# Rotary attention and routed feed-forward on one core: the row sums, their inverses and the division move by one step, and the kept copies of the feed-forward get fixed places

## The chip, the core and the metric

The kernel runs on one core of one Trainium2 chip. The metric is the device time of one execution in microseconds, and the figure given for a kernel is the median of its runs. Five engines work side by side, each with its own instruction stream in order: TensorE (PE, with its weight loads shown as PEld), VectorE (DVE), ScalarE (ACT), GpSimd (POOL) and SyncE (SP), which here only issues DMAs. They wait for each other through semaphores.

## The reference

The input is x, four sequences of 512 tokens with 512 features, all in fp32. It is normalised (layer norm), and two branches are added to x:

```python
def _L0_attn_ref(x, W_DQ, W_UQ, W_QR, W_DKV, W_UK, W_UV, W_KR, W_O):   # H=16, D_H=128, D_HR=64
    c_Q = x @ W_DQ.T                       # latent of 128
    q_C, q_R = heads(c_Q @ W_UQ.T), rope(heads(c_Q @ W_QR.T))
    c_KV = x @ W_DKV.T                     # latent of 128
    k_C, v = heads(c_KV @ W_UK.T), heads(c_KV @ W_UV.T)
    k_R = rope(x @ W_KR.T)                 # one for all heads
    scores = clip([q_C, q_R] . [k_C, k_R], -80, 80)
    weights = softmax(causal(scores) / sqrt(192))
    return (weights @ v) @ W_O.T

def _L0_ffn_ref(x, ...):                   # 7 experts of 512, top 3, and one shared
    output = (silu(x @ Ws1) * (x @ Wsg)) @ Ws2
    for e in range(7):
        output += ((silu(x @ W1[e]) * (x @ Wg[e])) @ W2[e]) * w_e[..., None]

x = x + attn(xn) + ffn(xn)
```

## The kernel before

The kernel has two large stages. First comes the feed-forward: norm, gate and shared expert, then the routed tokens, sorted by expert and cut into units of 512 rows. After it comes the attention, 16 heads of 4 sequences.

**Feed-forward.** A unit is three 512x512x512 products, called h, g and y. `product` does each with seven block products (a Strassen scheme) instead of eight, in the order `ORDER = (0, 1, 5, 4, 6, 2, 3)`; each is four matmuls. They go to three PSUM banks, `BANK = (0, 1, 2, 0, 2, 0, 0)`. A block product that another needs later is copied by ACT from its bank to SBUF (`kept`): product 0 gives v1, product 5 gives v2, product 4 gives v5 and product 6 gives v3. The bank is free for the next block product only after that copy. The copies live in one pool tag `v` with five buffers. In h, DVE adds v1, v2, v3 and v5 to other banks and ACT applies silu. In y, v1, v3 (with v5 added), v2 and a fourth tile v4 are stored by SP to DRAM (`y_d`), in the order v1, v3, v2, v4. A buffer that y stored is free again when that store has landed. The pool hands buffers out in the order in which they become free in the program. By the addresses of the built program, the h of the next unit gets these: v1 the buffer of y's v1, v2 that of y's v5 (which isn't stored), v5 that of y's v3, v3 that of y's v2. ACT runs in order, so a copy that waits for a buffer holds up those behind it.

**Attention.** The loop runs over 32 steps i; a step is one pair of heads of one sequence. The kernel works in latent space. Step i does:

- `scores(i)` on PE: score blocks without rotation (line 1432), then the rotary part onto them (line 1443). Banks: `a0`, `a1` for the first key block, `c` and one of the `pj` pool for the third, `b0` and `b1` for the second and fourth.
- `rotary_query(i+1)` (pqr, line 1282) and `query(i+1, 0)` (pq, line 1297) on PE for the next step.
- `weights(i)`: DVE clips the banks to SBUF (line 1461, six instructions), ACT takes exp (line 1465), POOL multiplies by the triangular mask (line 1469) and adds up key blocks into the tiles su (lines 1493 and 1497).
- `rope` on DVE for the next query: one product with cos and four with sin (lines 1268 and 1271), and a subtraction on POOL (line 1272).
- `values(i-1, j)` on PE (av, line 1513), copied by ACT into og.

A group q is four heads, those of steps 2q and 2q+1. For a group:

- `sums(q)`: four matmuls with ones (line 1532) into bank `a0` give the row sums, and DVE inverts them (line 1534, rc).
- `spread_by_dma(q)`: SP issues 16 DMAs of 64 KB that copy rc to four tiles rb of 128 partitions (line 1544).
- `divide(q)`: DVE multiplies og by the four rb (line 1566) and forms the block sums for the seven-product scheme (lines 1572 and 1575).
- `project_out(q)`: the product with the folded output weights m (op, line 230), 28 matmuls in seven block products into banks `b1`, `c` and `b0`. ACT copies some banks (line 1605), POOL adds the copies to acc (line 1612), and DVE adds three banks to acc (line 1615): bank `c` after the second block product, banks `b0` and `b1` at the end. `combine(g)` (line 1677, three DVE instructions) adds the routed rows of one token tile to acc; it stands right behind the first bank sum. `fetch` gathers the rows for a later combine with indirect DMAs from POOL (line 1664).

`keep` fixes the program's order on each engine for most instructions. So the order on DVE within two steps is what the source says. In the kernel before, with i even: clips, inverse of group i/2-1, rope, first bank sum, combine, two bank sums. With i odd: clips, rope, divide. `sums` stands behind pq of even steps, `project_out(q)` at the end of even step 2q+4.

Of the kernel before, what the change touches and what calls it, by code (L numbers as in the profile page):

```python
# [18 lines left out]
P = 128  # L19
# [23 lines left out]
def kernel(  # L43
# [87 lines left out]
    def rows(src):  # L131
        return src.rearrange("(c p) f -> p c f", p=P)

    def ffn_in(at, name, w, x_of, between, step=FC):

        hp = fps.tile([P, S], F32, tag="h", name=f"h_{name}")
        gp = fps.tile([P, S], F32, tag="g", name=f"g_{name}")
        for ps, wt in ((hp, w[0]), (gp, w[1])):
            for f in range(FC):
                for c in range(DC):  # L140
                    keep(
                        nc.tensor.matmul(
                            ps[:, ts(f, P)],
                            wt[:, c, ts(f, P)],
                            x_of(c),
                            start=(c == 0),
                            stop=(c == DC - 1),
                        )
                    )
            if ps is hp:  # L150
                between()
        sl = sw.tile([P, S], F32, tag="v", name=f"sl_{name}", bufs=5)
        keep(nc.scalar.activation(sl, hp, AF.Silu))
        cols = [t.rearrange("p (c n) -> p c n", c=FC) for t in (gp, sl)]

        for f in range(0, FC, step):
            keep(nc.vector.tensor_mul(*(t[:, f : f + step] for t in (at, *cols))))
        return at
# [113 lines left out]
    def block(t):  # L272
        if len(t.shape) > 2:
            axes = " ".join("abc"[: len(t.shape) - 1])
            t = t.rearrange(f"p {axes} -> p ({axes})")
        return t.rearrange("p (j f) -> p j f", j=2)
# [11 lines left out]
    def product(name, tag, a, w, done, hooks):  # L288

        banks = banks_of(tag, name)

        def kept(i, k):
            t = sw.tile([P, D], F32, tag="v", name=f"v{i}_{name}", bufs=5)
            keep(nc.scalar.copy(block(t), banks[k]))  # L297
            return block(t)

        copies = {0: (1, 0), 5: (2, 0), 4: (5, 2), 6: (3, 0)}  # L300
        sums = {1: 1, 2: 2, 3: 0}

        def then(p):
            if p in copies:
                done(copies[p][0], kept(*copies[p]))
            else:
                done(-p, banks[sums[p]])
            if p in hooks:
                hooks[p]()

        seven(a, w, banks, then, keep)
# [720 lines left out]
    def unit_out(s, a, w, hooks):  # L1032
        def to(t, n):
            at = (s * TPB + 2 * t) * P
            return y_d[at : at + 2 * P, half[n]].rearrange("(j p) f -> p j f", p=P)

        v = {}

        def done(i, src):
            v[i] = src  # L1040
            if i == -1:
                keep(V.tensor_add(v[1], src, v[1]))
                load_in(to(0, 0), v[1])
            elif i == 3:
                keep(V.tensor_add(v[3], v[3], v[5]))
                load_in(to(1, 1), v[3])
            elif i == -2:
                keep(V.tensor_add(v[2], src, v[2]))
                load_in(to(0, 1), v[2])
            elif i == -3:  # L1050
                t = block(sw.tile([P, D], F32, tag="v", name=f"v4_r{s}", bufs=5))
                keep(nc.scalar.copy(t, src))
                load_in(to(1, 0), t)

        product(f"yr{s}", "y", a, w, done, hooks)
# [324 lines left out]
    with tc.If(used < SURE + 1) as few:  # L1380
        at = act_tile("few").rearrange("p c (t f) -> p t c f", t=TPB)[:, 0]
        at = ffn_in(at, "few", wbuf, lambda c: xT[SURE][:, c, :P], nothing, 1)
        y = sw.tile([P, D], F32, tag="v", name="y_few", bufs=5)
        yp = ffn_out("few", at, wbuf, keep)
        keep(nc.scalar.copy(y[:, half[0]], yp[:, half[0]]))
        keep(nc.vector.tensor_copy(y[:, half[1]], yp[:, half[1]]))
        nc.sync.dma_start(y_d[ts(SURE * TPB, P), :], y)
    with few.Else():
        last[0] = None
# [63 lines left out]
    def weights(i, bank, then, behind):  # L1453

        pt = ap.tile([P, 5 * S], F32, tag="pt", name=f"pt_{i}")

        def clip(to, src):  # L1460
            keep(nc.vector.tensor_scalar(to, src, CLIP, -CLIP, ALU.min, ALU.max))  # L1461

        def exp(t):

            keep(nc.scalar.activation(t, t, AF.Exp, scale=QK_SCALE))  # L1465

        def mask(t, at, k=1, step=P):
            m = t[:, at : at + P]
            keep(nc.gpsimd.tensor_mul(m, m, tri))  # L1469

        for j in range(2):
            a = pt[:, ts(j, S)]
            clip(a, bank[j, 0])
            exp(a)
            mask(pt, PT[j, 0])
        half = 2 * P
        for j in (1, 0):
            clip(pt[:, PT[j, 2] : PT[j, 2] + half], bank[j, 2][:, :half])
        exp(pt[:, ts(2, S)])
        for j in range(2):  # L1480
            mask(pt, PT[j, 2])
        then()
        for j in range(2):
            t = pt[:, ts(3 + j, S)]
            clip(t, bank[j, 1])
            exp(t)
            mask(pt, PT[j, 1])
            mask(pt, PT[j, 3])
        behind()
        su = []  # L1490
        for j in range(2):
            t = ap.tile([P, S], F32, tag="su", name=f"su_{i}_{j}", bufs=4)
            keep(nc.gpsimd.tensor_copy(t[:, :P], pt[:, PT[j, 0] : PT[j, 0] + P]))
            for kc in range(1, TPB):
                prev = pt[:, PT[j, 0] + P : PT[j, 0] + S] if kc == 1 else t[:, kc * P :]
                keep(
                    nc.gpsimd.tensor_add(  # L1497
                        t[:, kc * P :], prev, pt[:, PT[j, kc] : PT[j, kc] + PT_W[kc]]
                    )
                )  # L1500
            su.append(t)
        pts[i], sus[i] = pt, su
# [25 lines left out]
    def sums(q):  # L1528

        sb = bank("a0")(f"sb_{q}")  # L1530
        for j, su in enumerate(sus.pop(2 * q) + sus.pop(2 * q + 1)):
            keep(nc.tensor.matmul(sb[ts(j, 32), :], ones[:, :32], su, start=True, stop=True))  # L1532
        rc = ap.tile([P, S], F32, tag="rc", name=f"rc_{q}", bufs=1)
        keep(nc.vector.reciprocal(rc, sb))
        return rc
# [21 lines left out]
    def divide(q):  # L1557

        o = og.pop(q)

        for cols in half if q == n // 2 - 1 else [slice(0, S)]:
            for j, rb in enumerate(spread[q]):
                keep(nc.vector.tensor_mul(o[:, j, cols], o[:, j, cols], rb[:, cols]))  # L1566
        a11, a21 = (o[:, 0:2, half[t]] for t in range(2))
        a12, a22 = (o[:, 2:4, half[t]] for t in range(2))
        x = [ap.tile([P, 2, S // 2], F32, tag=f"s{k}", name=f"s{k}_{q}") for k in (1, 2, 4)]

        def add(*t):
            keep(nc.vector.tensor_add(*t))

        def sub(*t):
            keep(nc.vector.tensor_sub(*t))

        firsts_of[q] = first_factors(add, sub, a11, a12, a21, a22, *x, a21)
# [104 lines left out]

    factors_of = {0: load_factors(0)}

    for i in range(n):
        more = i + 1 < n
        even = i % 2 == 0
        q = i // 2 - 1  # L1690
        held = scores(i)
        raw_copy, turn_q = rotary_query(i + 1, psum(f"pqr_{i + 1}")) if more else (nothing, nothing)
        qc_copy = query(i + 1, 0, psum(f"pq_{i + 1}_0")) if more else nothing
        weights(i, held, raw_copy, nothing if even else turn_q)
        qc_copy()
        if even and i > 0:
            spread_by_dma(q, sums(q))
        if even:
            turn_q()
        if i > 0:  # L1700
            values(i - 1, 0)
        if more:
            query(i + 1, 1, psum(f"pq_{i + 1}_1"))()
        if i < 2:
            project(2 + i, psum)
        if 1 < i < 5:
            turn_keys((2, 3, 1)[i - 2], psum)
        if i > 0:
            values(i - 1, 1)
        if even and i > 2:  # L1710
            project_out(q - 1, first_added=lambda: combine(q))
        if i == 1:
            combine(0)
        if even and i != 2 or i == 1:
            fetch((i + 1) // 2)
        if not even and i > 1:
            divide(q)

    q = n // 2 - 1

    def last_heads():
        combine(NTT - 1)
        values(n - 1, 0)
        values(n - 1, 1)
        last_rc.append(sums(q))

    last_rc = []
    project_out(q - 1, last_heads)
# [51 lines left out]
```

## Time and profile before

| | |
|---|---|
| Median of 10 runs | 1398.75 us (1387.89 to 1402.6) |
| The profiled execution: its own time / its span | 1386.11 us / 1384.3 us |
| Granted TensorE clock, mean of the span | 0.993 |
| Feed-forward units, 178.98 to 690.43 us: PE busy | 483.23 of 511.45 us |
| Attention loop, 842.09 to 1337.34 us: PE busy | 495.24 of 495.25 us |
| End, 1337.34 to 1384.3 us: PE busy | 42.44 of 46.96 us |

The share of busy time alone says little: matmuls are pipelined and their ends are modelled, so a PE that is shown busy throughout can still take longer than it must for a group of matmuls that waits inside. The median of the runs lies 12.6 us above the profiled execution's own time.

### The profile page before, as it was taken

To read this page: it belongs to the slowest core of one execution; us is meant where nothing else is said; L and a number is where in the kernel's file an instruction comes from. 1 tells how busy PE (TensorE), PEld (TensorE's weight loads), DVE (VectorE), ACT (ScalarE), POOL (GpSimd) and SP (SyncE) were. 2 spreads that over 40 slices of the span, in tenths; PEclk is the share of its full clock that TensorE was granted. 3 is DMA by queue.
4 is the path that set the end of the run, shared out by engine and by line. 5 is a ranking of instruction groups with operands and counts; after the bars stand their busy time and mean duration, and the time that the engine had idled before them with its cause. 6 is when DMAs were issued, how large, how long until landed. Compare 5 with 4: busy or idle time off the path is not lost.

```text
span 1384.3 us, 17913 instructions
## 1 busy us (share of the span) xinstructions
PE 1341.7 (97%) x5949; PEld 995.9 (72%) x5949; DVE 970.8 (70%) x1426; ACT 405.1 (29%) x714; POOL 844.5 (61%) x952
## 2 busy tenths in 40 slices
PE   9999899999999998999999999999999999999998
PEld 8778787788777786768755666666666666666666
DVE  7679455676656576648546877777977777987775
ACT  3234122222223221222223332332332332333231
POOL 5122654554436443343157888888888889888883
PEclk9999999999999999999999999999999999999999
DMA  7841245675557563443331123333123432124332
GB/s 274 207 128 31 78 127 152 166 207 171 172 152 213 160 187 111 126 141 111 99 108 31 46 86 105 107 100 116 54 87 101 137 107 90 48 87 128 107 107 84
DMA packets 174100, 167.90 MB, mean 121 GB/s; under 512 B 57904, under 2 KB 136752, under 8 KB 174000
## 3 DMA queue, kind: packets, MB, share of 16 engines
q1 hardware_dynamic: 161264, 133.10, 32.6%
q0 software_dynamic: 12736, 33.57, 8.1%
q8 instruction: 49, 0.80, 0.2%
q14 instruction: 51, 0.42, 0.1%
HBM read 116.02 MB, written 34.87 MB: 109 GB/s over the span
## 4 chain that ended last, share of the span: by engine, by line
PE 95%; issue 2%; DVE 1%; another core or an unknown queue 1%; ACT 1%; POOL 0%; DVEq 0%; ACTq 0%; POOLq 0%
PE op L230 14%; PE hr L230 11%; PE gr L230 10%; PE yr L230 10%; PE av L1513 10%; PE sb L1432 4%; PE sa L1432 4%; PE pq L1297 4%; PE sa L1443 2%; PE pqr L1282 2%; PE ys L230 2%; PE hs L230 2%; PE gs L230 2%; PE sb L1443 2%; PE sb L1532 2%
## 5 line engine op out<-in xcount | busy, mean ns | idle before, releaser
L182 POOL DMA_INDIRECT xs<-xn_d,idx_i x208 | 226.9, 1091 | 223.3 <-DVE xT L199 164.3
L1469 POOL TENSOR_TENSOR pt<-pt,tri 128x128 f32<-128x128 f32 x256 | 139.7, 566 | 68.7 <-ACT pt L1465 62.0
L1465 ACT ACTIVATE pt<-pt 128x512 f32<-128x512 f32 x160 | 94.4, 628 | 257.8 <-DVE pt L1461 255.2
L1513 PEld LDWEIGHTS av<-pt,xnT 128*128 128x128 f32 x512 | 95.4, 190 | 83.7 <-issue 47.7
L1513 PE MATMUL av<-pt,xnT 128*128 128x512 f32 (+3 forms) x512 | 149.8, 436 | 0.0
L230 PE MATMUL op<-m,og 128*128 128x256 f32 x512 | 118.6, 379 | 0.5 <-DVE og L1566 0.5
L1271 DVE TENSOR_TENSOR swap_q<-qraw,sinT 32x512 f32<-32x512 f32 x128 | 117.7, 920 | 1.7
L1497 POOL TENSOR_TENSOR su<-su,pt 128x256 f32<-128x256 f32 (+1 forms) x128 | 105.2, 822 | 10.0
L230 PEld LDWEIGHTS op<-m,og 128*128 128x128 f32 x512 | 96.0, 190 | 14.5 <-DVE og L1566 1.3
L1461 DVE TENSOR_SCALAR pt<-sa 128x512 f32<-128x512 f32 x64 | 41.0, 681 | 70.6 <-PE sa L1443 70.6
L1664 POOL DMA_INDIRECT yg<-y_d,pos_i x48 | 54.5, 1134 | 56.7 <-issue 50.3
L230 PE MATMUL op<-m,s 128*128 128x256 f32 x384 | 88.2, 379 | 0.1
L1497 POOL TENSOR_TENSOR su<-pt 128x384 f32<-128x384 f32 x64 | 83.8, 1310 | 0.0
L1612 POOL TENSOR_TENSOR acc<-acc,v 128x512 f32<-128x512 f32 x60 | 80.6, 1344 | 5.1 <-ACT v L1605 3.2
L230 PEld LDWEIGHTS op<-m,s 128*128 128x128 f32 x384 | 72.9, 190 | 10.3 <-issue 0.5
L230 PE MATMUL hr<-xT,w 128*128 128x256 f32 x288 | 68.1, 387 | 6.3 <-issue 6.3
L1677 DVE SCALAR_TENSOR_TENSOR acc<-yg,wk,acc 128x512 f32<-128x512 f32 x48 | 56.7, 1181 | 19.1 <-POOL acc L1612 17.9
L1605 ACT COPY v<-op 128x512 f32<-128x512 f32 x64 | 37.5, 586 | 108.3 <-PE op L230 94.6
L1566 DVE TENSOR_TENSOR og<-og,rb 128x512 f32<-128x512 f32 (+1 forms) x68 | 68.5, 1067 | 0.6 <-PE rb L1552 0.2
L230 PE MATMUL gr<-xT,w 128*128 128x256 f32 x288 | 67.3, 384 | 1.1 <-ACT v_gr L297 1.1
L230 PE MATMUL yr<-w,at_r 128*128 128x256 f32 x288 | 66.9, 380 | 0.3
L230 PEld LDWEIGHTS hr<-xT,w 128*128 128x128 f32 x288 | 55.5, 194 | 15.5 <-issue 7.9
(339 smaller groups left out, 2791.8 us busy)
## 6 DMA issues: line engine op xcount, KB each, us to landing
m<-m_d SPq DMA_DIRECT2D x112, 256.0 KB
w<-in_L_ffn_W_dram SPq DMA_DIRECT2D x52, 512.0 KB
rb<-rc SPq DMA_DIRECT2D x240, 64.0 KB
w<-in_L_ffn_Wg_dram SPq DMA_DIRECT2D x26, 512.0 KB
y_d<-v_yr SPq DMA_DIRECT2D x36, 256.0 KB
y_d<-none SPq DMA_DIRECT2D x24, 256.0 KB
acc<-in_L_attn_x_dram SPq DMA_DIRECT2D x16, 256.0 KB
xn_d<-xp SPq DMA_DIRECT2D x16, 256.0 KB
```

What stands on the lines that cost most here:

```text
L182: nc.gpsimd.indirect_dma_start(out=xs[blk][:, q, :], out_offset=None, in_=xn_d[:, :], in_offset=bass.IndirectOffsetOnAxis(ap=idx_i[:, q, b ...
L230: nc.tensor.matmul(banks[k][:, t, :], a[p][:, j, ts(t, P)], b[p][:, j, :], start=(k not in used), stop=(t == j == 1), skip_group_check=True,)
L1271: keep(nc.vector.tensor_mul(swap[there, :], raw[here, :], tables[1][here, :]))
L1297: keep(nc.tensor.matmul(ps, a_h[:, 2 * hp + j, :], lat(b, 0), start=True, stop=True))
L1432: nc.tensor.matmul(where(j, kc), lat(b, 1)[:, ts(kc, P)], qc[j][:, kc * P :], start=(kc != 3), stop=False,)
L1465: keep(nc.scalar.activation(t, t, AF.Exp, scale=QK_SCALE))
L1469: keep(nc.gpsimd.tensor_mul(m, m, tri))
L1497: nc.gpsimd.tensor_add(t[:, kc * P :], prev, pt[:, PT[j, kc] : PT[j, kc] + PT_W[kc]])
L1513: nc.tensor.matmul(av[:, kc * P :], lat(b, 3)[:, ts(kc, P)], pt[:, PT[j, kc] : PT[j, kc] + PT_W[kc]], start=(kc == 0), stop=(kc == TPB - 1),)
L1566: keep(nc.vector.tensor_mul(o[:, j, cols], o[:, j, cols], rb[:, cols]))
L1612: keep(eng.tensor_add(block, block, v))
L1677: nc.vector.scalar_tensor_tensor(acc[:, g, :], yg, wk[:, g, k : k + 1], acc[:, g, :], ALU.mult, ALU.add)
```

## The change

The diff has two parts that don't depend on each other.

**Feed-forward.** The one tag `v` with five buffers becomes five tags of one buffer each, va to ve, and a table says which copy goes to which: in h v1 and v5 to b, v2 to a, v3 to c; in g v1 to d, v2 to e, v5 to a, v3 to b; in y v1 to a, v2 to d, v5 to b, v3 to c, v4 to e. So the next unit's h gets: v1 the place of y's v5, v2 that of y's v1, v5 that of its own v1, v3 that of y's v3; the places of y's v2 and v4 go to g. Where only one block of rows is left, the copy of its result is one ACT instruction instead of half on ACT and half on DVE.

**Attention.** `sums(q)` moves from behind pq of even step 2q+2 to behind the rotary scores of odd step 2q+3, ahead of pqr. The inverse and the DMAs move to the end of that odd step's clips and rope. `divide(q)` moves from the end of odd step 2q+3 to even step 2q+4, behind its clips and ahead of its rope. `project_out(q)` stays at the end of even step 2q+4. For the last group of the loop (14), `sums` and the DMAs are in step 31 and `divide` follows the loop. The su tiles get six buffers instead of four; the block sums s1, s2, s4 get one each instead of two.

```diff
+    def place(k, name):
+        return sw.tile([P, S], F32, tag=f"v{k}", name=name)
+
+    PLACE = {"h": {1: "b", 2: "a", 5: "b", 3: "c"}, "g": {1: "d", 2: "e", 5: "a", 3: "b"}}
+    PLACE["y"] = {1: "a", 2: "d", 5: "b", 3: "c", 4: "e"}
...
         def kept(i, k):
-            t = sw.tile([P, D], F32, tag="v", name=f"v{i}_{name}", bufs=5)
+            t = place(PLACE[tag][i], f"v{i}_{name}")
...
-            t = ap.tile([P, S], F32, tag="su", name=f"su_{i}_{j}", bufs=4)
+            t = ap.tile([P, S], F32, tag="su", name=f"su_{i}_{j}", bufs=6)
...
             keep(nc.tensor.matmul(sb[ts(j, 32), :], ones[:, :32], su, start=True, stop=True))
+        return sb
+
+    def inverse(q, sb):
         rc = ap.tile([P, S], F32, tag="rc", name=f"rc_{q}", bufs=1)
...
-        q = i // 2 - 1
+        q = (i - 3) // 2
         held = scores(i)
+        if not even and q >= 0:
+            rc = sums(q)
...
         weights(i, held, raw_copy, nothing if even else turn_q)
         qc_copy()
-        if even and i > 0:
-            spread_by_dma(q, sums(q))
+        if not even and q >= 0:
+            spread_by_dma(q, inverse(q, rc))
+        if even and q >= 0:
+            divide(q)
         if even:
             turn_q()
...
-        if even and i > 2:
-            project_out(q - 1, first_added=lambda: combine(q))
+        if even and q >= 0:
+            project_out(q, first_added=lambda: combine(q + 1))
...
-        if not even and i > 1:
-            divide(q)
+    divide(q)
...
-        last_rc.append(sums(q))
+        last_rc.append(inverse(q, sums(q)))
```

More of the change, by code (lines that the diff above doesn't have):

```diff
@@ L151, in ffn_in @@
                 between()
-        sl = sw.tile([P, S], F32, tag="v", name=f"sl_{name}", bufs=5)
+        sl = place("ab"[name in ("s1", "s3")], f"sl_{name}")
         keep(nc.scalar.activation(sl, hp, AF.Silu))
@@ L1050, in done @@
             elif i == -3:
-                t = block(sw.tile([P, D], F32, tag="v", name=f"v4_r{s}", bufs=5))
+                t = block(place(PLACE["y"][4], f"v4_r{s}"))
                 keep(nc.scalar.copy(t, src))
@@ L1382 @@
         at = ffn_in(at, "few", wbuf, lambda c: xT[SURE][:, c, :P], nothing, 1)
[L1383 to L1386, printed above, removed]
+        y = place("b", "y_few")
+        keep(nc.scalar.copy(y, ffn_out("few", at, wbuf, keep)))
         nc.sync.dma_start(y_d[ts(SURE * TPB, P), :], y)
@@ L1568, in divide @@
         a12, a22 = (o[:, 2:4, half[t]] for t in range(2))
-        x = [ap.tile([P, 2, S // 2], F32, tag=f"s{k}", name=f"s{k}_{q}") for k in (1, 2, 4)]
+        x = []
+        for k in (1, 2, 4):
+            x.append(ap.tile([P, 2, S // 2], F32, tag=f"s{k}", name=f"s{k}_{q}", bufs=1))
         def add(*t):
```

## The prediction

> **What bounds the kernel now.** I read the page first, then busy time by stage, the chain of waits inside the attention loop, and the order of time around one even step and around one feed-forward unit.
>
> ```profile
> PE 1341.7 (97%) x5949; PEld 995.9 (72%) x5949; DVE 970.8 (70%) x1426; ACT 405.1 (29%) x714; POOL 844.5 (61%) x952
> PE 95%; issue 2%; DVE 1%; another core or an unknown queue 1%; ACT 1%; POOL 0%; DVEq 0%; ACTq 0%; POOLq 0%
> ```
>
> PE ends last nearly everywhere. In the loop DVE (79% busy) and POOL (84%) come close, so their queues matter as soon as work is shifted within a pair of steps. The chain of waits shows one even step with its sums, and the first sums of the kernel:
>
> ```profile
> 752.33 1.00 PE sb L1532 x8
> ...
> 897.12 1.72 PE sa L1432 x4
> ...
> 903.79 1.05 PE pqr L1282 x2
> 904.84 0.86 PE pq L1297 x2
> 905.70 0.01 issue
> 905.71 1.57 PE sb L1532 x8
> 907.27 2.35 PE av L1513 x8
> ...
> 912.64 12.09 PE op L230 x56
> ```
>
> At 752.33 the sums cost 1.00 us, in the loop 1.46 to 1.57: there they wait for the clip that empties bank a0 and for POOL's last su. The av behind them takes 2.35, elsewhere 2.16. An odd step takes 13.76 (883.36 to 897.12), a pair 41.27 (842.09 to 1337.34 is twelve pairs).
>
> The same step in the order of time, on DVE and SP:
>
> ```profile
> 896.47 4.46 DVE L1566 TENSOR_TENSOR og<-og,rb 128x512 f32<-128x512 f32 x4
> 904.98 1.27 DVE L1461 TENSOR_SCALAR pt<-sa 128x512 f32<-128x512 f32 x2
> 908.03 3.34 DVE L1534 RECIPROCAL rc<-sb 128x512 f32<-128x512 f32 x1
> 911.40 10.01 SPq L1544 DMA_DIRECT2D rb<-rc  x16
> 912.10 4.08 DVE L1271 TENSOR_TENSOR swap_q<-qraw,sinT 32x512 f32<-32x512 f32 x4
> 916.82 4.38 DVE L1677 SCALAR_TENSOR_TENSOR acc<-yg,wk,acc 128x512 f32<-128x512 f32 x3
> 924.82 1.29 DVE L1615 TENSOR_TENSOR acc<-op,acc 128x512 f32<-128x512 f32 x2 [3.61 <-POOL acc L1612]
> ```
>
> The divide ends at 905.0 and delays the clips: they begin 7.9 after the step's start, in odd steps 5.4. But the 16 copies, issued from 911.4 on, aren't read before the next divide at 937.7, 26 us later. That slack is what the change spends.
>
> In the feed-forward PE idles 28.2 of 511.45 us. The rows around one unit's h:
>
> ```profile
> 226.86 0.58 ACT L297 COPY v_hr<-hr 128x512 f32<-128x512 f32 x1 [3.05 <-PE hr L230]
> 227.50 1.99 PE L230 MATMUL hr<-xT,f 128*128 128x256 f32 x8 [1.42 <-issue]
> 230.36 1.99 PE L230 MATMUL hr<-xt_r,w 128*128 128x256 f32 x8 [0.88 <-issue]
> ```
>
> PE starts 0.06 after a late ACT copy ends. That copy is h's v5, whose buffer held y's v3, stored from 214.5 on.
>
> **Feed-forward places.** PE's idle before h's matmuls is 20.4 us in all. By unit, the gaps behind a late v5 or v3 are 2.30, 2.36, 1.64, 2.35, 2.35 and 3.11: 14.1. The others (1.34, 1.69, 0.54, 2.71) stand behind a late v2, whose buffer had long been read; I leave them. In the new table v5 takes the place of its own unit's v1, and only v3 waits for y's v3. In these units that store let v5 go at the latest 0.9 after the sixth block product's end; PE needs bank 0 1.72 after that end, and a copy takes 0.58. So no gap is left. Gain 14, bounds 0 (the copies were late for another reason) and 21.5 (all gaps, and 1.07 before a gr). The copy of the last block by ACT alone costs 0.58 for two halves side by side: +0.3 at most, behind 1.03 of idle.
>
> **Sums on PE.** Removed from the even step: 1.46 and 0.19 of the av, 1.65. Added in the odd step: 1.0, between 0.86 (two records of pq) and 1.57. Their su are a step old. Bank a0 is empty in time: the first clip starts 1.1 after the rotary scores (888.76 against 887.67), takes 0.65, and the sums come at 2.36. So PE alone would need 41.27 - 0.65 = 40.6 a pair.
>
> [...]
>
> **Division on DVE.** In the changed program's instruction order, DVE has clips, rope, inverse in the odd step; clips, four products, four factor sums, rope, first bank sum, combine, two bank sums in the even one. The last of these free b0 and b1, which the next odd step's scores need 2.58 after its start (883.36 to 885.94). This closes a loop. From the release of b0:
>
> - PE: rest of the plain scores 1.73, rotary 2.36, sums 1.0, then pqr's start to the rope's 1.97 (890.03 to 892.00): 7.1.
> - Rope 4.47 (892.00 to 896.47). Inverse 3.27 (908.03 to 911.30).
> - Copies: 16 issues take 10.01. For the first group DMA traffic goes on to 768.3 or a little beyond, 11.4 after the first issue at 756.9. No row shows the landing itself. Between 11.4 and 12.1; I take 11.8, the end of traffic with a little for the semaphore.
> - Last product 1.1, factor sums 4.0 (900.97 to 904.98). Both are shorter when POOL is quiet (0.77 and 3.0); POOL adds su then, so I take the long ones.
> - Rope 4.5: between 4.47 and 4.88, the short one, since POOL's su are mostly done.
> - First bank sum 0.6, combine 4.4; POOL beside it runs rope subtraction and two adds at 1.72, 5.2 in all; then 0.65 for the bank sum that frees b0: 5.85.
>
> Sum 42.1 (39.6 with all short ends, 42.9 with the long ones), above PE's 40.6 and 0.8 above 41.27. The wait that is late next is the last rb, then b0.
>
> Every fourth group (4, 8, 12) its combine touches the rows of bank sum one, so it waits for POOL, and POOL issues two gathers ahead of the add that the last bank sums need. The rows of such a step: bank sum 957.49, last sums 966.21, 8.7, of which 1.07 is POOL's su backlog, which the later rope hides. So 7.7 + 0.65 = 8.4 instead of 5.85: 44.6, +3.3.
>
> Within an even step op's third block product wants the second factor sum: it stands at 3.44 behind op's start, and the chain delivers it some 0.3 late. That delay overlaps with the wait for b0 and isn't counted again.
>
> Over the loop: ten pairs x 0.8 = 8, three x 3.3 = 10. The first pair (759.13 to 800.84, group 0) ends some 1.6 late by the same sum.
>
> **The end.** Group 14's sums stood in step 30; now they are in step 31, with nothing behind them that could cover the copies. From the sb scores of step 31: clips end at 6.1 (1339.76 to 1345.88), inverse 9.4, last rb 21.1, product 22.1, two factor sums 23.8. Op's third block product started at 1351.81, 12.05 after those scores. So 11.7 later (bounds 10.5 and 12.5), with PE idle, and the rest follows.
>
> **Sum.** -14 + 0.3 + 1.6 + 8 + 10 + 11.7 = +17.6: 1386.1 becomes 1403.7 in a profiled execution. I carry the difference to the median, 1398.75: 1416, +1.3%.
>
> **Rivals.**
>
> *Faster.* The copies land soon enough. If the loop's sum falls below 40.6, which needs 1.5 less than I take, DVE no longer ends last and PE gains 0.65 on ten pairs. For: POOL may be quiet during the products and factor sums (2.3 are at stake), and all late h copies may be due to the stores. Against: POOL is 84% busy. Then -6.5 + 3 x 1 - 1 + 11 - 21 = -14.5: 1384.
>
> *No difference.* The loop keeps its 41.27 except for the three slow groups (+2.5 each), and the places give 20: 7.5 + 11.7 - 20 = -1: 1398.
>
> *Places without effect.* The late copies wait for something else than the stores: +31 stays, 1430. For: four gaps stand behind a copy whose buffer was free. Against: the gaps recur behind v5 and v3, the two that wait for late stores.
>
> **How the numbers follow.** Forecast 0.56, places without effect 0.20, no difference 0.13, faster 0.11. About 0.5% (7 us) is what a measurement of this kernel can tell from no change; 1416 and 1430 lie beyond it. So faster 0.11, same 0.13, slower 0.76. The range runs from just below no difference (1396) to 1434, with the long ends of the loop beside places without effect.
>
> **What would show it.** Right: PE idle before op at the end of about 10 us, and DVE waiting for rb there; in the loop a wait of PE's sb scores for DVE's bank sums (line 1615 before), 1.5 us in ordinary pairs and about 4 in pairs of groups 4, 8, 12; sums near 1.0 and av 2.16 behind them; no gaps of 1.4 and 0.9 in h. Wrong: loop pairs near 40.6, or DVE never idle before a product with rb; h gaps as before; a new wait of PE or ACT in the shared expert, where POOL reads the fixed places.

## The result and the profile after

| | before | after |
|---|---|---|
| Median of the runs | 1395.28 us (62 runs) | 1450.91 us (17 runs) |
| Ratio, 95% interval | | 1.0385 [1.0364, 1.0406] |
| Profiled execution: own time / span | 1386.11 / 1384.3 us | 1450.18 / 1448.4 us |
| Granted clock, mean of the span | 0.993 | 0.976 |

The change costs 55.6 us. The direction is as forecast, the size is three times the forecast, and above its range. In the numbering of the changed kernel lines lie 6 to 11 higher: scores 1438 and 1449, clips 1467, sums 1538, inverse 1543, copies 1553, products with rb 1575, bank sums 1626, POOL's adds 1623, gathers 1675.

The page of the profile after: busy time, shares of the chain, and the group of the first scores (its last columns are busy time, mean ns, idle time ahead of it and what ended most of that):

```profile
PE 1361.2 (94%) x5949; PEld 1007.2 (70%) x5949; DVE 958.6 (66%) x1425; ACT 407.8 (28%) x714; POOL 831.5 (57%) x952
PE 75%; DVE 12%; issue 4%; SPq 3%; another core or an unknown queue 2%; POOL 2%; ACT 1%; DMA 1%; POOLq 0%; DVEq 0%; ACTq 0%
L1438 PE MATMUL sa<-qc,xnT 128*128 128x512 f32 x128 | 71.1, 684 | 31.8 <-DVE rc L1543 30.9
```

PE's share of the chain fell from 95% to 75%, and DVE's rose from 1% to 12%. The third line names the place: PE is idle for 30.9 us ahead of the first scores sa, waiting for the inverse rc. No step of the prediction has this wait. The chain of waits shows two of the 14 places (start, duration, what):

```profile
863.28 0.99 PE sb L1538 x8
...
870.18 3.37 DVE rc L1543
873.55 0.04 issue
873.59 3.59 PE sa L1438 x4
...
914.89 3.37 DVE rc L1543
918.26 0.04 issue
918.30 1.98 PE sa L1438 x4
```

The sums are written to bank a0 at 863.28, in 0.99, as assumed. The bank is free again only when the inverse has read it, at 873.55, and the inverse stands behind the odd step's clips and rope on DVE. But the first instruction of the next even step is a score block in bank a0. PE was through with the odd step at 871.36 and waited 2.23, at the next place 2.24.

The chain has a second surprise. The same four matmuls take 1.72 without a wait, 1.98 at 918.30 and 3.59 at 873.59. Busy time by stretches, around these two places (columns: length, busy time and count of PE, PEld, DVE, ACT, POOL, then the granted clock, DMA share and GB/s):

```profile
871.30:873.50 2.20, 0.06 (x1) 0.00 (x0) 2.20 (x1) 0.59 (x1) 2.12 (x4) 0.99 0.00 0
873.50:875.00 1.50, 1.41 (x2) 0.84 (x3) 0.04 (x1) 0.00 (x0) 1.42 (x4) 0.50 0.16 40
875.00:877.00 2.00, 2.00 (x3) 0.67 (x2) 0.00 (x0) 0.00 (x0) 1.45 (x3) 0.54 0.40 101
877.00:879.00 2.00, 2.00 (x9) 1.48 (x8) 0.00 (x0) 0.00 (x0) 0.00 (x0) 1.00 0.39 98
...
916.00:918.30 2.30, 0.07 (x1) 0.00 (x0) 2.25 (x1) 0.59 (x1) 2.18 (x4) 1.00 0.00 0
918.30:920.00 1.70, 1.70 (x4) 0.87 (x5) 0.00 (x0) 0.00 (x0) 1.64 (x3) 1.00 0.15 39
```

After the first wait the granted clock is 0.50 for 3.4 us, after the second it stays at 1.00. So ordinary pairs take 43.1 us, or 44.8 where the half clock follows the wait: here every second one.

In groups 4, 8 and 12 the forecast wait for DVE's bank sums is there as well, behind the copies and POOL's gathers:

```profile
968.54 2.02 DMA rb<-rc
...
985.93 1.27 POOL acc L1623
...
988.26 1.35 POOL yg L1675
...
991.07 1.28 POOL acc L1623
...
992.38 0.70 DVE acc L1626
...
993.12 2.00 PE sb L1438 x8
```

The end, from step 31's score blocks sb to the last group's block products:

```profile
1391.31 1.73 PE sb L1438 x8
...
1394.15 3.12 DVE pt L1467 x6
1397.28 3.27 DVE rc L1543
...
1409.99 2.04 DMA rb<-rc
...
1412.15 0.70 DVE og L1575
1412.90 6.61 PE op L238 x22
```

And the feed-forward, in the order of time (the last bracket is the idle time ahead and what ended it):

```profile
219.69 0.69 DVE L333 TENSOR_TENSOR at_r<-hr,v_hr 128x512 f32<-128x512 f32 x1 [1.87 <-issue]
220.28 3.62 PE L238 MATMUL hr<-xt_r,f 128*128 128x256 f32 x16
227.87 0.59 ACT L305 COPY v_hr<-hr 128x512 f32<-128x512 f32 x1 [5.08 <-remote]
228.51 3.57 PE L238 MATMUL hr<-xT,f 128*128 128x256 f32 x8 [2.88 <-issue]
```

The copy v5 at 227.87 now writes the place that DVE finished reading at 220.38, and no store is involved. Its block product is shown to end at 223.90. It still starts 4 us later, and PE waits for it. PE's waits ahead of h are 27.7 us after and 20.4 before. The semaphore events in the two traces say more: PE's own signal for that block product comes at 227.85, 0.02 ahead of the copy. In the kernel before it comes at 226.83, 2.5 behind the shown end, with the copy at 226.86; there the store of y's v3 lands at 226.82, so that trace alone can't tell the store from PE. Of the twelve copies v5 of a trace, 8 start 1.8 us or more behind the shown end of their block product before, and 9 after, where none of them needs a store.

**Where the time went, by stage.** From the start of one odd step to the next, from the two traces:

| | before | after | difference | forecast |
|---|---|---|---|---|
| up to the first scores | 702.79 | 711.13 | +8.3 | -13.7 |
| first two pairs of the loop | 77.72 | 79.19 | +1.5 | +1.6 |
| the other 13 pairs | 536.50 | 578.07 | +41.6 | +18 |
| from step 31 to the end | 47.12 | 59.81 | +12.7 | +11.7 |

The attention makes 55.7 of it, as much as the medians differ. The +8.3 lies in the feed-forward, whose gaps differ widely between executions, as the run of the places alone shows.

### The profile page after: what moved, and what is told of

It is laid out like the page before. It is cut to its first block, busy times and chain, and to the rows that moved or that the text cites. A ratio compares the mean times of both kernels' runs of the same rounds, so it can differ in the third digit from the quotient of the medians.

```text
span 1448.4 us, 17933 instructions
## 1 busy us (share of the span) xinstructions
PE 1361.2 (94%) x5949; PEld 1007.2 (70%) x5949; DVE 958.6 (66%) x1425; ACT 407.8 (28%) x714; POOL 831.5 (57%) x952
## 4 chain that ended last, share of the span: by engine, by line
PE 75%; DVE 12%; issue 4%; SPq 3%; another core or an unknown queue 2%; POOL 2%; ACT 1%; DMA 1%; POOLq 0%; DVEq 0%; ACTq 0%
PE op L238 10%; PE yr L238 10%; PE gr L238 10%; PE hr L238 10%; DVE swap_q L1279 4%; PE av L1519 4%; PE sa L1438 3%; PE sb L1438 3%; DVE rc L1543 3%; SPq L1553 3%; PE ys L238 2%; PE hs L238 2%; PE sa L1449 2%; PE gs L238 2%
## 5 line engine op out<-in xcount | busy, mean ns | idle before, releaser
L1475 POOL TENSOR_TENSOR pt<-pt,tri 128x128 f32<-128x128 f32 x256 | 158.1, 639 | 111.1 <-ACT pt L1471 106.6
L1519 PEld LDWEIGHTS av<-pt,xnT 128*128 128x128 f32 x512 | 96.7, 190 | 79.0 <-issue 54.9
L238 PE MATMUL op<-m,og 128*128 128x256 f32 x512 | 122.3, 387 | 8.0 <-issue 4.3
L238 PEld LDWEIGHTS op<-m,og 128*128 128x128 f32 x512 | 97.6, 194 | 23.9 <-DVE og L1575 5.9
L1438 PE MATMUL sa<-qc,xnT 128*128 128x512 f32 x128 | 71.1, 684 | 31.8 <-DVE rc L1543 30.9
L1503 POOL TENSOR_TENSOR su<-su,pt 128x256 f32<-128x256 f32 (+1 forms) x128 | 94.9, 742 | 10.0
L1623 POOL TENSOR_TENSOR acc<-acc,v 128x512 f32<-128x512 f32 x60 | 84.7, 1421 | 20.1 <-DVE acc L1626 12.3
L1503 POOL TENSOR_TENSOR su<-pt 128x384 f32<-128x384 f32 x64 | 76.3, 1192 | 0.0
L1616 ACT COPY v<-op 128x512 f32<-128x512 f32 x64 | 37.5, 586 | 120.0 <-PE op L238 120.0
L238 PEld LDWEIGHTS hr<-xT,w 128*128 128x128 f32 x288 | 56.2, 197 | 20.5 <-issue 12.7
L1688 DVE SCALAR_TENSOR_TENSOR acc<-yg,wk,acc 128x512 f32<-128x512 f32 x48 | 59.9, 1248 | 14.0 <-POOL acc L1623 12.8
```

The costliest lines, as they stand in the source:

```text
L238: nc.tensor.matmul(banks[k][:, t, :], a[p][:, j, ts(t, P)], b[p][:, j, :], start=(k not in used), stop=(t == j == 1), skip_group_check=True,)
L1438: nc.tensor.matmul(where(j, kc), lat(b, 1)[:, ts(kc, P)], qc[j][:, kc * P :], start=(kc != 3), stop=False,)
L1503: nc.gpsimd.tensor_add(t[:, kc * P :], prev, pt[:, PT[j, kc] : PT[j, kc] + PT_W[kc]])
L1519: nc.tensor.matmul(av[:, kc * P :], lat(b, 3)[:, ts(kc, P)], pt[:, PT[j, kc] : PT[j, kc] + PT_W[kc]], start=(kc == 0), stop=(kc == TPB - 1),)
L1623: keep(eng.tensor_add(block, block, v))
L1688: nc.vector.scalar_tensor_tensor(acc[:, g, :], yg, wk[:, g, k : k + 1], acc[:, g, :], ALU.mult, ALU.add)
```

## The experiments

Two theories. **A**: bank a0, held until the inverse has read it, holds up PE at each even step. **B**, the prediction's loop: the copies land too late for the division, and the release of banks b0 and b1 sets the pace. The runs came in four batches, on three chips. The kernel before took 1340.5, 1340.3 and 1340.3 us in the first three batches and 1370 in the last, so each run is compared with the kernel before of its own batch, and pairs are compared by the traces: the attention of the kernel before takes 681.5 us in the first trace, and 681.4 at 1340, in the run of the places alone, where it is unchanged. The expectations of the first batch (the inverse ahead of the rope, the copy by ACT, the last group, the places) are on the scale of the first result, where the changed kernel took 1451 and the kernel before 1395; it is the distance from these that counts.

**The changed kernel again.** Nothing is altered.

> The changed kernel, unaltered, beside the kernel before on whichever chip these runs get. In the first result's two traces the attention alone (from the few stage's end on) is 55.65 us longer, the feed-forward up to there 8.5. If the difference belongs to the attention, as theory A has it, and the feed-forward's share is only the h gaps' own scatter, it is 55.6 above the kernel before here too, wherever the kernel before stands (1396 beside 1340.5). If the feed-forward places cost something, 60 or more.

1397.04 beside 1340.31, +56.7, ratio 1.0429 [1.0413, 1.0445]. So the cost belongs to the attention and is the same where the kernel is 55 us faster. 1397.04 is what the next runs are read against, also those of the batch at 1340.5, which had no run of the changed kernel.

**The inverse ahead of the rope.**

```diff
+        def behind():
+            if q >= 0:
+                spread_by_dma(q, inverse(q, rc))
+            turn_q()
-        weights(i, held, raw_copy, nothing if even else turn_q)
+        weights(i, held, raw_copy, nothing if even else behind)
...
-        if not even and q >= 0:
-            spread_by_dma(q, inverse(q, rc))
```

> The changed kernel with one thing moved: in odd steps the inverse and the 16 copies stand right behind the clips, ahead of the rope. Theory A (bank a0 is held by the sums until the inverse, which stands behind the rope, has read it; the next even step's first scores wait 2.24 us for it, and at the lowered clock behind that idle time they lose another 0.3 or 1.7): the inverse ends some 4.2 earlier, 2 before those scores, so wait and lowered clock go, and ordinary pairs fall from 43.1 and 44.7 to 40.6 to 41. With nine such pairs, three slow groups at about 42 (their copies land 4.5 earlier too) and 4 from the first pair: about 1407. Theory B (the copies land too late for the division, and the loop over banks b0 and b1 sets the pace): the copies too come 4.5 earlier, so it expects a gain as well, but at most 2 a pair: 1420 to 1425.

1359.57, +19.1, ratio 1.0141 [1.0125, 1.0157]: 37.5 below the changed kernel, where theory A expected 44 and theory B 26 to 31. The wait for rc and the low clock are gone from the loop. Ordinary pairs take 41.62, though, not 40.6 to 41. The order of time around one sb says why:

```profile
837.59 1.01 POOL L1675 DMA_INDIRECT yg<-y_d,pos_i  x1 [0.30 <-issue]
838.63 1.28 POOL L1623 TENSOR_TENSOR acc<-acc,v 128x512 f32<-128x512 f32 x1
839.94 1.29 DVE L1626 TENSOR_TENSOR acc<-op,acc 128x512 f32<-128x512 f32 x2 [2.82 <-POOL acc L1623]
840.69 2.00 PE L1438 MATMUL sb<-qc,xnT 128*128 128x384 f32 x8 [0.76 <-DVE acc L1626]
```

POOL's order isn't written out by hand there. In the changed kernel two gathers stand ahead of POOL's second add in groups 0, 4, 8 and 12 only; in this build, as in the kernel before, they do in every group, and DVE's bank sums wait for that add.

**ACT copies the sums out of the bank.** The copies to rb start as late as in the changed kernel.

```diff
+    def moved(q, sb):
+        t = ap.tile([P, S], F32, tag="rc_in", name=f"rcin_{q}", bufs=1)
+        keep(nc.scalar.copy(t, sb))
+        return t
...
-            spread_by_dma(q, inverse(q, rc))
+            spread_by_dma(q, inverse(q, moved(q, rc)))
```

> The changed kernel, but ACT copies the sums from bank a0 to SBUF behind the exps of the odd step, and the inverse, still behind the rope, reads that copy. The bank is free some 4 us earlier (about 3 before the next even step's scores), the 16 copies start as late as in the changed kernel. So the two theories part here. Theory A alone (only the bank holds up PE): ordinary pairs 40.6 to 41, slow groups about 44, 1408 to 1412. Theory B (the late copies set the pace once the bank is free, as the prediction had it): ordinary pairs 42.1, groups 4, 8 and 12 44.6, about 1427. If neither holds, 1450.

1362.97, +22.5, ratio 1.0167 [1.0151, 1.0184]: 34.1 below the changed kernel, between theory A (39 to 43) and theory B (24). The ordinary pairs decide: they take 40.76 or 40.60, as A has it. So bank a0, with the low clock behind its wait, cost the ordinary pairs 2.5 to 4.2 us, and the late copies cost them at most 0.16. Seven of fifteen pairs take 42.2 to 45; groups 4, 8 and 12 stand at 44.98, 43.35 and 43.46, the first with 3.41 us at half clock behind a wait for the bank sums. One ordinary pair gives the loop of theory B in full, since here DVE does wait for rb:

```profile
853.44 3.35 DVE L1548 RECIPROCAL rc<-rcin 128x512 f32<-128x512 f32 x1
856.82 10.02 SPq L1558 DMA_DIRECT2D rb<-rc  x16
868.36 0.84 DVE L1580 TENSOR_TENSOR og<-og,rb 128x512 f32<-128x512 f32 x1 [1.61 <-DMA rb<-rc]
877.00 0.69 DVE L1631 TENSOR_TENSOR acc<-op,acc 128x512 f32<-128x512 f32 x1
882.20 1.28 DVE L1631 TENSOR_TENSOR acc<-op,acc 128x512 f32<-128x512 f32 x2
```

From the release of b0 at 842.09 to the next at 882.85 it is 40.76.

**The same with the gathers behind POOL's four adds.**

```diff
-            keep(
-                nc.gpsimd.indirect_dma_start(
+            with after_last(nc.gpsimd):
+                nc.gpsimd.indirect_dma_start(
```

(`after_last` issues an instruction behind the engine's last one so far.)

> e4_sums_copied_by_act with the same move of the gathers. There the copies go out as late as in the changed kernel, and the pairs are 40.76 or 40.6 when ordinary, but six of fifteen take 42.2 to 45 (16.5 us above 40.7 together). By the prediction's term for groups 4, 8 and 12 (two gathers ahead of the add that the last bank sums need) these lose 2.4 each: 1363 - 8 to 12 = 1351 to 1355. If the late copies themselves are the cause, it stays within 2 of 1363.

1352.9, +12.6, ratio 1.0095 [1.0079, 1.011], inside the expectation, though not by its term of 2.4 a group. The largest pair is now 42.25. Two pairs fell by 3.0, group 4 one of them; each had a stretch of half clock that went as well. Groups 8 and 12 fell by 1.35 and 1.40, to 42.0, and the end by 1.7. So the gathers' place made about half of the excess of groups 8 and 12; the rest is a wait of sb for the bank sums that stays (3.4 us in three groups).

**The last group as before**, on top of the inverse ahead of the rope: group 14's sums, inverse and copies stand in step 30 behind the division.

```diff
+        if i == n - 2:
+            spread_by_dma(q + 1, inverse(q + 1, sums(q + 1)))
```

> As e1_inverse_first, and the last group of the loop (14) is treated as in the kernel before: its sums, inverse and copies stand in step 30, behind that step's division, instead of in step 31. Expected by theory A: the end after the loop (59.7 us in the changed kernel, 46.96 before) falls by 11.7 to 12.7, since the copies have step 31 to land in; step 30 grows by some 1.5. About 1396, within 0.5% of the kernel before. Theory B would keep its loop term: 1410. If the division of group 13 and the inverse of group 14 in one step delay the rope too much, the end gains only half: 1402.

1350.69, +10.2, ratio 1.0079 [1.0063, 1.0095]. From 61.37 in the run with the inverse ahead, the end falls to 49.99, by 11.4; the pair of step 30 grows from 42.20 to 43.38. That is the end's term, nearly as expected.

**All of it: the gathers behind the adds as well.** Inverse ahead of the rope, last group early, gathers last.

> e2_inverse_first_last_group_early, with POOL's three gathers of each even step behind its four adds to acc instead of between them. In e2's chain an ordinary pair (41.62) is set by copies, division, rope, POOL's rope subtraction, two gathers, an add and DVE's two bank sums, after which PE's sb scores start 0.76 late. Theory: the gathers are 2.4 of that chain, so the wait of the sb scores goes, ordinary pairs come to 40.6 to 40.8 and groups 4, 8 and 12 to 41: 1350.7 - 13 = 1338, 0.2% below the kernel before. Rival (POOL is as late anyway, since its total is the same): 1350.

1333.56, 6.8 below the kernel before, ratio 0.9953 [0.9939, 0.9967]: 0.5%, a small gain but clear of the interval. It is 4.4 below the expected 1338, since the end fell as well, by 2.7. Ordinary pairs take 40.60, groups 4 and 8 40.83, and no wait of PE is left in the loop:

```profile
842.79 0.99 PE sb L1538 x8
843.78 1.06 PE pqr L1290 x2
844.84 0.86 PE pq L1305 x2
845.70 2.16 PE av L1519 x8
```

The move of the sums is worth 0.66 a pair (41.26 to 40.60), once nothing waits for it. The av takes 2.16 instead of 2.35 where the sums no longer precede it, and the forecast 0.65 had this 0.19 in it. pqr takes 1.06 behind the sums and 1.05 behind the 64-row scores, against 0.86 for pq, which is of the same size; the cause was not shown.

**The places alone.** The kernel before with the feed-forward part of the diff only.

```diff
-            t = sw.tile([P, D], F32, tag="v", name=f"v{i}_{name}", bufs=5)
+            t = place(PLACE[tag][i], f"v{i}_{name}")
```

> The kernel before with the fixed places of the kept copies (and the few block copied by ACT alone) as the only change. By the prediction's step (the late copies v5 and v3 in h wait for buffers that y stores): -14, 1381. By its rival (they wait for something else: in the changed kernel's trace v5 needs no store and still starts 2 to 4 us after its block product's end, when the semaphore of PE moves): 1395, within 3 us of the kernel before.

1340.07 beside 1340.49, ratio 0.9999 [0.999, 1.0008]. The places do nothing measurable there. But the trace tells more. All waits of PE in the feed-forward, first of the kernel before in the first result, then of this run (us in total, times, the longest):

```profile
PE hr L230 <- issue: 20.4, 15, 2.7
PE gr L230 <- ACT v_gr L297: 7.6, 2, 6.5
```

```profile
PE y_few L170 <- DVE at_few L163: 0.5, 1, 0.5
```

In this run there are no gaps in h at all, and the first scores start at 656.69 instead of 702.79. That isn't the places' doing, since the kernel before beside it is as fast: gaps and time come and go with the batch. Whether it is the chip or the time of the run that matters was not tested. So this run can't show whether the places close a gap. The two traces of the first result have the gaps, and the places closed none there: v5 starts as late without a store.

**Filling the wait.** Does the idle time bring the low clock? Matmuls that nobody reads, at the end of each odd step:

```diff
+        if not even and q >= 0 and more:
+            fill = bank("c")(f"fill_{i}")
+            for _ in range(5):
+                keep(nc.tensor.matmul(fill, lat(0, 1)[:, :P], lat(0, 0), start=True, stop=True))
```

> The changed kernel with five more matmuls (128x512, 0.43 us each, into bank c, read by nobody) at the end of each odd step, where PE waits 2.24 us for bank a0. The wait for the inverse stays as it is, but PE is not idle in it. Theory (every second such idle time is followed by 3.5 us at half the granted clock, which costs 1.6 to 1.7): the pairs of 44.7 become 43.1 or less, seven times 1.6 = 11 below the changed kernel of the same call. Rival (the slow first scores have another cause than the idle time): no gain, or 2 us of loss from the added matmuls.

1420.69, +80.4, ratio 1.0594 [1.0578, 1.0611]: a miss. I had sized the fill by one record a matmul; a 128x512 matmul has two of 0.43, and the five took 4.29, 2.05 more than the wait. In eleven groups sb also waits for a bank sum, 9.4 us in all. Pairs take 45.92. Every sa behind the fill takes 1.72, so the clock stayed up. Shorter, with two of 512 columns and one of 256 (2.15 us):

> As e7_filled_wait, with the fill cut to what PE waits: e7 showed that a 128x512 matmul is two records of 0.43, so its five took 4.29, 2.05 more than the wait of 2.24. Here two of 512 columns and one of 256: 2.15. Theory (the idle time, not the bank, brings the slow first scores): each pair loses 2.24 to the inverse as before but runs at the full clock behind it: 43.1 to 43.2 in all ordinary pairs, where the changed kernel had 44.79 in eleven of twelve on the second chip; 11 x 1.65 = 18 less than 1397, so 1379 beside a kernel before of 1340. Rival (no link between the idle time and the clock): 1397.

1395.15, +54.9, ratio 1.0411 [1.0392, 1.043]: the time didn't fall. No stretch at half clock is left in the loop, but in this build POOL's gathers stand ahead of the second add in every group, and the bank sums set pairs of 44.1 to 44.9. That is the prediction's loop for groups 4, 8 and 12 (44.6), now in all groups. Two more runs put the gathers behind the adds, by the change above, with the shorter fill and without a fill:

> As e8_shorter_fill, with POOL's gathers behind the four adds. In e8 the low clock was gone from the loop (no interval at half clock in it, the changed kernel has nine), but its pairs were 44.1 to 44.9: there POOL's two gathers stood between the first two adds in every group, the bank sums waited for them and the sb scores started 0.76 to 1.01 late. With the gathers out of that chain: all pairs 43.1 to 43.2 (41.27 less 0.65 for the sums plus 2.24 behind the inverse plus 0.3), 1395 - 15 = 1380. If the fill itself costs the rest, 44 and 1395.

> The changed kernel with the gathers behind the adds and nothing else, as the partner of e9: bank a0 is still held until the inverse behind the rope, and PE is idle there. Theory A: ordinary pairs stay at 44.8 (half clock behind the wait) or 43.1 (full clock), groups 4, 8 and 12 fall from 46.4 or 44.8 to the same: at most 8 below the changed kernel's 1397, 1389 to 1397; the difference to e9 is what the low clock costs, 10 to 17 us. If the gathers were the main loss in the changed kernel, 1375 or less.

With the fill: 1402.97, +33.0, ratio 1.0268 [1.0186, 1.0351]. Without: 1421.81, +51.8, ratio 1.04 [1.0325, 1.0475]. Here the kernel before scattered from 1359.5 to 1380.2, hence the wide intervals, and the first of the two is unclear by time alone; the attention by the traces takes 721.4 and 736.3. With the fill every ordinary pair takes 43.10; without it 43.10 or 44.79. One place of each, first with the fill, then without:

```profile
872.64 3.37 DVE rc L1543
...
876.05 1.98 PE sa L1438 x4
```

```profile
887.00 3.37 DVE rc L1543
890.37 0.04 issue
890.41 3.63 PE sa L1438 x4
```

The wait for rc is the same; the slow first scores go with the idle time. So the low clock costs an ordinary pair 1.69.

## Why the prediction was wrong, step by step

**Sums on PE: the step that failed.** Its price was right (0.99 for 1.0, and 40.60 a pair for 40.6 where nothing else waits). What failed is the sentence "Bank a0 is empty in time": it asked when the sums may write the bank and not when the next user gets it back. That user is the first instruction of the next even step. The times for it stood in the prediction: the rope ended 8.8 after the rotary scores began (887.67 to 896.47), and PE was through with the odd step at 9.45 (897.12). The sums put both back by 1.0, and the inverse adds 3.27 behind the rope: 13.1 against 10.45, 2.6 late. In the trace of after it was 2.24; the shorter rope (4.2 for 4.47) makes 0.27 of the difference.

Measured for the 13 pairs: 13 x (2.24 + 0.25 - 0.65) = 23.9, with 0.25 by which the first scores run longer after a wait (1.98 for 1.72); 7 x 1.69 = 11.8 for the low clock; 3 x 1.6 = 4.8 for the bank sums in groups 4, 8 and 12; and 1.2 in the first of these pairs, whose sb scores also wait for a bank sum. The sum is 41.7, measured 41.6, forecast 18.

**The loop over b0.** The mechanism is there, the size was off. With bank a0 out of the way the ordinary loop takes 40.76 (forecast 42.1): the second rope 3.7 for 4.5, the copies 11.54 for 11.8, the last product 0.84 for 1.1, the first rope 4.2 for 4.47. I had taken the long end of the last product, on the ground that POOL adds su beside it, and had no row of a rope as short as 3.7. The prediction put the short ends at 39.6 and the long ones at 42.9; the terms listed for it come to 40.3 and 42.8. In the changed kernel itself this loop decides in groups 0, 4, 8 and 12 alone: elsewhere PE comes so much later to the even step that the copies have landed. In groups 4, 8 and 12 it adds 1.6 to the a0 wait. Without that wait they take 43.4 and 43.5, and 45.0 with the half clock, where the forecast was 44.6 (+3.3).

**The end.** Forecast +11.7, measured +12.7, by the path as told: from the sb scores the clips end at 5.97 (6.1), the inverse at 9.24 (9.4), the last rb is there at 20.7 (21.1). The 1 us more lies behind that: the 22 matmuls of op from 1412.90 take 6.61, at full clock 22 x 0.216 = 4.75 (56 of them take 12.09 in the loop before). The clock is at 0.5 from 1405.92 to 1416.16 there, behind PE's idle time of 4.33 up to 1405.23; the prediction had no term for it.

**The first pair.** Forecast +1.6, measured +1.5 for the first two together, but by luck. The pair without a group lost 1.2, since its sums moved on, and the one of group 0 took 2.7 more, with a wait of 1.84 for bank a0 and one of 0.71 for POOL's rope subtraction. The wait for b0, on which the forecast rested, comes a pair later.

**Feed-forward places.** Forecast -13.7, measured nothing: -0.4 in the run of the places alone, and in the first result the attention accounts for all that the medians differ by. The step that failed is that v5 is late because it waits for the store of y's v3. The gap of 4 us between a block product's shown end and its copy stays when the place needs no store, and the copy follows PE's own signal. "Places without effect" was right on this, at 0.20; its total, 1430, lacked the wait for a0. What makes PE signal late stays open: the batches at 1340 showed nothing of it.

**Rivals.** "Faster" needed copies that land soon enough. They nearly did: the loop without the a0 wait comes within 0.2 of PE's own time. It failed on the bank, and on the 21 us that it took from the places. "No difference" needed 20 from the places and a loop of 41.27, and neither came.

## What to carry to other kernels

When an operation moves into a shared bank, ask two questions: when the bank is empty for it, and who writes it next and what must have read it by then. The second is answered on the reader's queue: here a 3.3 us inverse behind a 4.2 us rope cost 2.2 us of idle TensorE a pair, and putting it ahead of the rope took 37.5 us out of 56.7. A removed wait shows the next one at once, and this may be the order that a scheduler gave to another engine: read it after every build.

## What the runs showed of the hardware

**A short idle time of TensorE can cost nearly as much again.** In the loop of the first result the scores sa wait for rc 14 times, first for 1.84 us and then 13 times for 2.23 or 2.24. Behind 7 of these 13 idle times the granted clock was 0.5 for 3.41 us; behind the other 6, and behind the first, it stayed at 1. The starts of the 7 stretches are 44.37 or 88.75 us apart, 13 or 26 times 3.41. They lie between 0.15 us ahead of the end of the wait and 0.97 behind it. Idle times of this length elsewhere did not all bring the low clock: in the feed-forward of the same trace it stayed at 1 behind the two of 2.28 us that ended at 274.51 and 363.05. In the run with the gathers behind alone, too, the clock was 0.55 in the 2.0 us behind the wait that ended at 890.4 and 1.00 behind the one that ended at 935.2. What decides between the two was not shown. That the idle time brings the low clock rests on the fill: with it, no stretch at 0.5 is left in the loop.

**The feed-forward of one and the same kernel took 54 us more in one batch than in another.** The changed kernel came to its first scores at 711.1 us in the first result and at 656.8 when run again, while its attention took 737.3 and 739.2. In the first result PE waits 27.7 us ahead of h. In the run with the inverse ahead of the rope, which has the same feed-forward and its first scores at 656.6, PE's one wait from 178 to 656 us is 0.5, in the few rows' block.
